# A convolution and an involution on one core: the pixel weights' layout, from [group, tap row] to [pair of groups, tap row, group of the pair]

## The chip, the cores and the metric

The kernel runs on one core of a Trainium2 chip. The metric is the device time of one execution in microseconds, the median of three runs. Names: PE is TensorE (PEld its weight load), DVE is VectorE, ACT is ScalarE, POOL is GpSimd, SP is the sync engine, which here only issues DMAs. SBUF is the on-chip memory of 128 partitions, PSUM the memory that matmuls write to, HBM (DRAM) the memory outside.

## The reference

The input `x` is [32, 256, 32, 32] in fp32: 32 images, 256 channels, 32 x 32 pixels. Two layers, each a group norm with 32 groups of 8 channels, an operator, and a residual:

```python
# layer 0: 3x3 convolution, 256 -> 256, on values rounded to fp16
x = x + _L0_conv_ref(_gn(x), L0_conv_weight, L0_conv_bias)
# layer 1: involution, K = 7, G = 16 groups of GC = 16 channels
y = relu(bn(einsum('oc,bchw->bohw', w1, xn)))            # 64 channels
w = einsum('oc,bchw->bohw', w2, y) + b2[None, :, None, None]
w = w.reshape(b, G, K * K, H, W)                          # 16 x 49 weights for each pixel
out = einsum('bgkhw,bgckhw->bgchw', w, patches)           # 7 x 7 patches, zero padded
x = x + out
```

In the involution each pixel has its own 49 weights for each of the 16 groups, and the 16 channels of a group share them.

## The kernel before

**Layer 0.** `front(b)` is a generator with the steps of one image: the group norm's sums (L219, ACT) and its small DVE operations (L227 to L235), the convolution as 18 fp16 matmuls for each half of the pixels and each half of the channels (L332), rounding to fp16 on DVE (L346), bias and residual (L348), the second group norm, the 64 channels `y` (L380, L387), and sixteen transposes of 128 x 128 (L395), copied into `pixels` by ACT (L399).

**The pixel weights.** `weights(b, r0)` makes the 7 x 7 x 16 weights of four image rows. With 32 columns of `y` as the stationary operand, a matmul (L410) gives the weights of 32 pixels: 16 groups for two tap columns `dj`, up to 224 numbers. Four of them, for different pairs of tap columns, fill 128 partitions. DVE then adds the bias `b2_sb` and writes the result from PSUM to the ring `w_sb` (L428); this is called the eviction here. The ring has one place for every output row, and in a place [group, tap row] with WIN = 10 tap rows, since an input row of a window of 4 rows can take part in 10 output rows. The place for a tap row depends on the row distance, so the eviction writes a diagonal: the offset `K1 - 1 - d0` and steps `[WB, rows], [WB - 1, d1 - d0], [WIN, G]`. The innermost step, over the groups, is WIN = 10 words. `ring_pieces` cuts an eviction where the ring wraps or the image ends, which gives the shapes of 224, 192, 128, 64 and 16 elements.

**The way through DRAM.** `scatter(b, k, part)` (L477, on SP) writes the ring's rows to `wd` in DRAM, 640 bytes for each pixel, row and tap column. In `wd` a pixel has WPIX = 7 * 160 + 4 words. `load_bands(b, k)` (L490) reads them back with partitions as input pixels: 16 DMAs for eight image rows, each of 16 rows of WPIX words; 14 are issued by POOL and two by SP. In the source, the row step `ROW - 1` shifts each row of pixels by one tap row, so that all pixels of a band line up. Three band buffers take turns.

**The sums.** `sums(b, m)` (L515) multiplies, for a window of 4 rows by 19 columns of pixels, `pixels` (stationary, 64 partitions x 32 channels, of which 16 are zero) with a slice of the band (moving), accumulating in `acc` in PSUM. For a group the moving operand is [19 pixels, up to 10 tap rows]; the 10 tap rows are adjacent words in SBUF and the pixels 160 words apart. Each fp32 matmul of the program runs as two MATMUL instructions, so a window takes 64. `add_windows` (L531, DVE) adds `acc` to `x`, and `store` (SP) writes the result.

**The order** is written out by hand: a loop over half-steps `n`, 16 for each image, in which sums, windows, weights (18 half-steps ahead), scatters, x loads and band loads (9 ahead) are placed by fixed distances. Each engine works its queue in that order.

Of the kernel before, what the change touches and what calls it, by code (L numbers as in the profile page):

```python
# [9 lines left out]
F32 = mybir.dt.float32  # L10
AF = mybir.ActivationFunctionType
ALU = mybir.AluOpType

P = 128
# [6 lines left out]
K1, PAD1 = 7, 3  # L21
TAPS = K1 * K1
CR = 64
G = 16
# [12 lines left out]
XR = 4  # L37
RG = 2
KP = P // RG
TR = RG * XR  # L40
SIDES = 2
JC = W // SIDES
K = H // TR
M = K * SIDES
WIN = XR + K1 - 1
WINC = JC + K1 - 1
WINI = JC + PAD1

WB = G * WIN
WPIX = K1 * WB + XR
SW = K1 * G
S = H + 2 * PAD1
T = 4
TW = P // T
PAIR = 3 * GC
PAIRS = G // 2
ROW = S * WPIX  # L60
WR = 4
NBAND = 3
SHARE = 8
NPIX = 6
RING = 24
# [6 lines left out]
def tile_quant_conv_then_involution(  # L72
# [16 lines left out]
    nc = tc.nc  # L89
    PSUM = bass.MemoryType.PSUM  # L90

    const = ctx.enter_context(tc.tile_pool(name="const", bufs=1))
# [45 lines left out]
        nc.gpsimd.memset(t, 0.0)  # L138

    y_sb = [const.tile([P, N // 2], F32, name=f"y_{i}") for i in range(2)]  # L140
    bands = [const.tile([P, SIDES, WINC * WB + XR], F32, name=f"band_{i}") for i in range(NBAND)]
    for t in bands[CH:]:
        nc.gpsimd.memset(t, 0.0)
    pixels = [const.tile([P, 2, PAIRS, PAIR], F32, name=f"pixels_{i}") for i in range(NPIX)]
# [1 line left out]
        nc.gpsimd.memset(t, 0.0)  # L146


    w_sb = const.tile([P, 2, RING, G, WIN], F32, name="w_sb")
    wd = dram.tile([H, S, WPIX], F32, name="wd")  # L150
    acc = [ps_acc.tile([P, RG, NT], F32, name=f"acc_{d}") for d in range(SIDES)]

# [6 lines left out]
    w2_sb = const.tile([P, K1, SW], F32, name="w2_sb")  # L159
    for i in range(2):  # L160
        nc.sync.dma_start(w2_sb[i * CR : (i + 1) * CR], w2)
    b2_sb = const.tile([P, 2, SW], F32, name="b2_sb")
    for dj in range(K1):
        t, e = divmod(dj, 2)
        nc.sync.dma_start(b2_sb[t * TW : (t + 1) * TW, e], b2[dj].partition_broadcast(TW))

    bias_sb = const.tile([P, CH], F32, name="bias_sb")
    nc.sync.dma_start(bias_sb, bias0.rearrange("(h p) -> p h", p=P))
# [15 lines left out]


    for col, cols, at, n in (
        (0, S, K1 * WB, XR),
        (PAD1, PAD1, 0, PAD1 * WB),
        (W, PAD1, (K1 - PAD1) * WB, PAD1 * WB),
    ):  # L190
        to = bass.AP(
            tensor=wd.tensor,
            offset=wd.offset + col * WPIX + at,
            ap=[[ROW, H], [WPIX, cols], [1, n]],
        )
        nc.sync.dma_start(to, bands[NBAND - 1][:H, 0, :n].unsqueeze(1).to_broadcast([H, cols, n]))
# [205 lines left out]
    def weights(b, r0):  # L402

        pws = [ps_w.tile([P, 2, 2, SW], F32, tag=f"pw{i}", name=f"pw{i}") for i in range(2)]
        for r in range(2):
            for t in range(T):
                for i in range(2):
                    half = slice(i * CR, (i + 1) * CR)
                    dj = slice(2 * t, min(2 * t + 2, K1))
                    nc.tensor.matmul(  # L410
                        pws[i][t * TW : (t + 1) * TW, r, : dj.stop - dj.start],
                        y_sb[b % 2][half, (r0 // 2 + r) * W : (r0 // 2 + r + 1) * W],
                        w2_sb[half, dj],
                        start=True,
                        stop=True,
                    )
        for i in range(2):
            for e in range(2):
                p = P if e == 0 else (K1 // 2) * TW
                for r, rows, d0, d1, at in ring_pieces(b, r0 + 2 * i):  # L420

                    to = w_sb[:p, e]
                    to = bass.AP(
                        tensor=to.tensor,
                        offset=to.offset + at * WB + K1 - 1 - d0,
                        ap=[to.ap[0], [WB, rows], [WB - 1, d1 - d0], [WIN, G]],
                    )
                    nc.vector.tensor_tensor(  # L428
                        to,
                        pws[i][:p, r : r + rows, e, d0 * G : d1 * G].rearrange("p r (d g) -> p r d g", g=G),  # L430
                        b2_sb[:p, e, d0 * G : d1 * G]
                        .unsqueeze(1)
                        .to_broadcast([p, rows, (d1 - d0) * G])
                        .rearrange("p r (d g) -> p r d g", g=G),
                        ALU.add,
                    )

    def ring_pieces(b, r0):

        def place(r, d):
            s = r0 + r + d - PAD1
            return (b * H + s) % RING if 0 <= s < H else None

        def together(d):
            return place(0, d) is not None and place(1, d) == place(0, d) + 1

        pieces = []
        for rows, ok in (  # L450
            ((0, 2), together),
            ((0, 1), lambda d: place(0, d) is not None and not together(d)),
            ((1, 1), lambda d: place(1, d) is not None and not together(d)),
        ):
            d = 0
            while d < K1:
                d0 = d
                while d < K1 and ok(d) and place(rows[0], d) == place(rows[0], d0) + d - d0:
                    d += 1
                if d > d0:  # L460
                    pieces.append((*rows, d0, d, place(rows[0], d0)))
                else:
                    d += 1
        return pieces

    def scatter(b, k, part):

        at = (b * H + k * TR) % RING
        for dj in range(part, K1, 2):
            t, e = divmod(dj, 2)  # L470
            to = bass.AP(
                tensor=wd.tensor,
                offset=wd.offset + k * TR * ROW + dj * WPIX + (K1 - 1 - dj) * WB,
                ap=[[WPIX, TW], [ROW, TR], [1, WB]],
            )
            rows = w_sb[t * TW : (t + 1) * TW, e, at : at + TR]
            nc.sync.dma_start(to, rows.rearrange("p s g r -> p s (g r)"))  # L477

    def load_bands(b, k):

        band = bands[(b * K + k) % NBAND]
        for i in range(JC):
            j = i // 2 + i % 2 * JC // 2
            src = bass.AP(
                tensor=wd.tensor,
                offset=wd.offset + k * TR * ROW + (j + PAD1) * WPIX,
                ap=[[ROW - 1, TR], [JC * WPIX, SIDES], [1, WPIX]],
            )
            queue = nc.sync if i % SHARE == SHARE - 1 else nc.gpsimd
            queue.dma_start(band[j::JC, :, j * WB : j * WB + WPIX], src)  # L490

    def windows(b, m):


        k, d = divmod(m, SIDES)
        for g in range(RG):
            top = k * TR + g * XR - PAD1
            at = acc[d][:, g, : CH * WINI * WIN].rearrange("p (h j r) -> p h j r", h=CH, r=WIN)
            yield g, at, top, max(top, 0), min(top + WIN, H)

    def sums(b, m):

        k, d = divmod(m, SIDES)
        j0 = 0 if d else PAD1
        band = bands[(b * K + k) % NBAND][:, d]
        px = pixels[(b * K + k) % NPIX][:, d]
        for h in range(CH):
            for v in range(2):
                for g, at, top, f, l in windows(b, m):
                    p = slice(g * KP, (g + 1) * KP)  # L510
                    of = band[p, g * XR + j0 * WB : g * XR + (j0 + WINI) * WB]
                    of = of.rearrange("p (j g r) -> p j g r", g=G, r=WIN)
                    for t in range(T):
                        a = h * T + t
                        nc.tensor.matmul(  # L515
                            at[t * TW : (t + 1) * TW, h, :, f - top : l - top],
                            px[p, a, v * GC : v * GC + TW],
                            of[:, :, 2 * a + v, f - top : l - top],
                            start=(h, v) == (0, 0),
                            stop=(h, v) == (CH - 1, 1),  # L520
                        )
# [20 lines left out]
    def due(n, lag):  # L542

        b, i = divmod(n - lag, per)
        return (b, i) if 0 <= b < B else (None, None)

    with tc.manual_schedule():
        fronts = {}
        for n in range(FRONT, B * per + 2):
            b, i = due(n, FRONT)  # L550
# [12 lines left out]
            b, i = due(n, 0)  # L563
            if b is not None and i % 2 == 0:
                sums(b, i // 2)
            b, i = due(n, 1)
# [6 lines left out]
            b, i = due(n, 2)  # L573
            if b is not None and i == 2 * (M - 1 - SIDES):
                store(b, 0)
            b, i = due(n, -LEAD)
            if b is not None and i % 2 == 0:
                weights(b, i // 2 * WR)

            for part in range(2):  # L580
                b, i = due(n, -LEAD + 1 + part)
                if b is not None and i % 2 == 0:
                    for k in range(K):
                        if i // 2 == min((k + 1) * TR // WR, H // WR - 1):
                            scatter(b, k, part)
            b, i = due(n, LOAD)
# [3 lines left out]
            b, i = due(n, 3 - 4 * NBAND)  # L590
            if b is not None and i % 4 == 0:
                load_bands(b, i // 4)
# [37 lines left out]
```

## Time and profile before

| | |
|---|---|
| median of three runs | 1392.44 us |
| lowest, highest | 1381.25, 1393.82 us |
| profiled execution, span from first to last instruction | 1387.9 us |
| busy in the span: PE, DVE, ACT, POOL | 1250.5, 934.7, 727.6, 1007.6 us |
| DMA, mean rate | 266 GB/s, 369 MB |
| evictions (L428): busy, count | 455.5 us, 1920 |
| sums (L515): busy, count | 411.6 us, 16,384 |

The profile is of one execution, whose own time is given only as its span. "Busy" counts time in which an engine had an instruction at work; instructions of one engine can overlap, so the mean duration of a group times its count can exceed its busy time. A group's row has, after the bar, busy time, mean duration in ns, and the idle time just before, with what ended it. A row of waits reads: engine, operation and line, what ended the wait, total us, times, longest us. "issue" is time in which the engine waited for nothing that the profile shows.

### The profile page before, as it was taken

What the parts mean: (1) busy time and instruction counts of PE and PEld (TensorE: products, weight loads), DVE (VectorE), ACT (ScalarE), POOL (GpSimd) and SP (SyncE); (2) the same over time, 40 slices, a digit from 0 to 9 for tenths busy, and PEclk for the clock granted to TensorE, in tenths of its full rate; (3) what the DMA queues carried; (4) which work ended last, traced back from release to release, by engine and by line L of the source; (5) the groups of instructions that cost most, each with busy time, mean ns of one, the idle gap of its engine ahead of it and who ended that gap; (6) DMA issues with size and microseconds to landing.
All of it is one profiled execution on the core that took longest, in us unless ns stands there. A gap on an engine that the chain in (4) does not pass through costs nothing.

```text
span 1387.9 us, 70012 instructions
## 1 busy us (share of the span) xinstructions
PE 1250.5 (90%) x29440; PEld 798.5 (58%) x29440; DVE 934.7 (67%) x3179; ACT 727.6 (52%) x1699; POOL 1007.6 (73%) x1818
## 2 busy tenths in 40 slices
PE   2899999899899999998899999899999999999665
PEld 1356555566565665655565666566566655666543
DVE  4467776677767776776576677667777776677652
ACT  4866555465645555655455555545565654653300
POOL 8057777777787777767777787776876777778785
PEclk9999999999999999999999999999999999999986
DMA  6079999999999998999999999999999999999995
GB/s 217 1 195 286 283 277 283 284 266 292 287 277 274 287 294 254 285 279 269 273 275 286 289 275 279 288 277 264 288 283 272 295 285 279 280 280 272 280 269 162
DMA packets 366232, 369.33 MB, mean 266 GB/s; under 512 B 78624, under 2 KB 308192, under 8 KB 365664
## 3 DMA queue, kind: packets, MB, share of 16 engines
q1 hardware_dynamic: 279904, 235.72, 57.5%
q0 software_dynamic: 86016, 129.14, 33.8%
q8 instruction: 234, 3.83, 1.2%
q14 instruction: 78, 0.64, 0.1%
HBM read 183.81 MB, written 180.74 MB: 263 GB/s over the span
## 4 chain that ended last, share of the span: by engine, by line
PE 55%; DMA 25%; DVE 5%; issue 5%; POOL 4%; SPq 3%; ACT 3%; POOLq 0%; DVEq 0%; ACTq 0%
PE pc L332 22%; PE acc L515 17%; DMA band<-wd 14%; PE pw L410 10%; DMA wd<-w_sb 8%; POOL band L490 4%; PE py L380 3%; DVE w_sb L428 3%; SPq L477 3%; PE pt L395 2%; DMA out<-x 1%; ACT junk L219 1%; DVE x L531 1%; DMA band<-in_w 1%; ACT xn L278 0%
## 5 line engine op out<-in xcount | busy, mean ns | idle before, releaser
L490 POOL DMA_DIRECT2D band<-wd x1792 | 978.0, 548 | 364.1 <-DMA band<-wd 225.3
L428 DVE TENSOR_TENSOR w_sb<-pw,b_sb 128x16 f32<-128x16 f32 (+9 forms) x1920 | 455.5, 349 | 359.2 <-PE pw L410 345.4
L332 PE MATMUL pc<-xq,wq 128*128 128x496 f16 (+3 forms) x2304 | 536.4, 379 | 32.5 <-ACT xq L278 28.0
L515 PE MATMUL acc<-band,pixels 64*32 64x190 f32 (+1 forms) x16384 | 411.6, 322 | 80.2 <-DMA band<-wd 44.6
L332 PEld LDWEIGHTS <-wq 128*128 128x128 f16 x2304 | 206.8, 98 | 328.2 <-issue 113.0
L515 PEld LDWEIGHTS acc<-band,pixels 64*32 64x32 f32 x16384 | 296.1, 108 | 165.1 <-issue 100.1
L410 PE MATMUL pw<-w_sb,y 64*32 64x224 f32 (+1 forms) x8192 | 291.2, 332 | 15.1 <-issue 13.9
L531 DVE TENSOR_TENSOR x<-acc,x 128x380 f32<-128x380 f32 (+1 forms) x512 | 261.7, 511 | 33.6 <-PE acc L515 24.6
L410 PEld LDWEIGHTS pw<-w_sb,y 64*32 64x32 f32 x8192 | 180.6, 106 | 45.7 <-issue 28.8
L399 ACT COPY pixels<-pt 128x512 f32<-128x512 f32 x128 | 73.6, 575 | 224.0 <-PE pt L395 224.0
L219 ACT ACTIVATE junk<-x 128x512 f16<-128x512 f32 (+1 forms) x192 | 146.5, 763 | 18.0 <-DVE x L348 9.6
L219 ACT ACTIVATE junk<-x,mean 128x1024 f16<-128x1024 f32 x128 | 147.1, 1149 | 4.3
L250 ACT ACTIVATE s<-back,eps 128x2 f32<-128x2 f32 x64 | 18.9, 296 | 207.3 <-DVE back L235 207.2
L346 DVE TENSOR_SCALAR q<-pc 128x512 f16<-128x512 f32 x128 | 87.2, 682 | 19.2 <-PE pc L332 19.0
L278 ACT ACTIVATE xn<-x,off,rstd 128x512 f32<-128x512 f32 x128 | 96.1, 800 | 0.0
L348 DVE SCALAR_TENSOR_TENSOR x<-q,bias_sb,x 128x512 f32<-128x512 f16 x128 | 92.0, 719 | 0.2
L395 PEld LDWEIGHTS pt<-ident,xn 128*128 128x128 f32 x512 | 63.9, 142 | 27.7 <-issue 3.3
L395 PE MATMUL pt<-ident,xn 128*128 128x128 f32 x512 | 78.0, 275 | 1.5 <-ACT pixels L399 1.5
L240 ACT ACTIVATE mean<-back 128x2 f32<-128x2 f32 x64 | 12.7, 198 | 120.6 <-DVE back L235 120.6
L278 ACT ACTIVATE xq<-x,off,rstd 128x1024 f16<-128x1024 f32 x64 | 75.5, 1226 | 0.0
L380 PEld LDWEIGHTS py<-xn,w_sb 128*64 128x64 f32 x2048 | 62.7, 138 | 16.7 <-issue 8.3
L380 PE MATMUL py<-xn,w_sb 128*64 128x64 f32 x2048 | 67.5, 224 | 2.8 <-ACT xn L278 1.8
(40 smaller groups left out, 374.5 us busy)
## 6 DMA issues: line engine op xcount, KB each, us to landing
wd<-w_sb SPq DMA_DIRECT2D x896, 160.0 KB
band<-wd POOLq DMA_DIRECT2D x1792, 70.2 KB, 4.9
x<-in_x SPq DMA_DIRECT2D x64, 512.0 KB
out<-x SPq DMA_DIRECT2D x64, 512.0 KB
band<-wd SPq DMA_DIRECT2D x256, 70.2 KB
band<-in_w SPq DMA_DIRECT2D x2, 1152.0 KB
w_sb<-in_w SPq DMA_DIRECT2D x2, 196.0 KB
wd<-band SPq DMA_DIRECT2D x2, 180.0 KB
```

What stands on the lines that cost most here:

```text
L219: nc.scalar.activation(junk[:, n0:n1], src[:, h, n0:n1], func, bias=bias, accum_out=self.sums[:, i : i + 1])
L278: nc.scalar.activation(dst, src, AF.Identity, bias=self.off[:, one], scale=self.rstd[:, one])
L332: nc.tensor.matmul(pc.rearrange("p (r c) -> p r c", c=W)[:, r0 - nt * RT : r1 - nt * RT, c0:c1], wq[:, kh, k, mh * P : (mh + 1) * P], xq[: ...
L346: nc.vector.tensor_scalar(q, pc, F16_MAX, -F16_MAX, ALU.min, ALU.max)
L348: nc.vector.scalar_tensor_tensor(xt[:, mh, cols], q, bias_sb[:, mh : mh + 1], xt[:, mh, cols], ALU.add, ALU.add)
L380: nc.tensor.matmul(py[i * CR : (i + 1) * CR, cols], w1_sb[:, kh, :], px[:, r : r + 2], start=kh == 0, stop=kh == CH - 1,)
L395: nc.tensor.transpose(pt[:, i, h * P : (h + 1) * P], xn[:, h, (m + i) * P : (m + i + 1) * P], ident)
L410: nc.tensor.matmul(pws[i][t * TW : (t + 1) * TW, r, : dj.stop - dj.start], y_sb[b % 2][half, (r0 // 2 + r) * W : (r0 // 2 + r + 1) * W], w ...
L428: nc.vector.tensor_tensor(to, pws[i][:p, r : r + rows, e, d0 * G : d1 * G].rearrange("p r (d g) -> p r d g", g=G), b2_sb[:p, e, d0 * G : d ...
L490: queue.dma_start(band[j::JC, :, j * WB : j * WB + WPIX], src)
L515: nc.tensor.matmul(at[t * TW : (t + 1) * TW, h, :, f - top : l - top], px[p, a, v * GC : v * GC + TW], of[:, :, 2 * a + v, f - top : l - top],
L531: nc.vector.tensor_tensor(x_at, of, x_at, ALU.add)
```

## The change

In `w_sb`, `wd` and the bands, the 160 numbers of a place are no longer [16 groups, 10 tap rows] but [8 pairs of groups, 10 tap rows, 2 groups of the pair]. So:

- The eviction's innermost step is two adjacent words; its loops are rows and pairs together, tap rows, and the two groups. For that, the matmul L410 writes its rows to other places in PSUM (row inside tap column), the host reorders the columns of `w2` and `b2` by pair, tap row, group, and the bias is held twice, once for each row, which takes 14 loads of `b2` where there were seven.
- One tap row is now two words, so the shift between rows in `load_bands` is `ROW - V` with V = 2, the band's second half of the partitions starts V * XR words in, and the padding grows from 4 to 8 words: a pixel has 1128 words in place of 1124.
- The sums read one group of a pair: the 10 tap rows are every second word.

```diff
+V = 2
+A = G // V
 WB = G * WIN
-WPIX = K1 * WB + XR
+PAD = V * (TR - XR)
+WPIX = K1 * WB + PAD
...
-    w_sb = const.tile([P, 2, RING, G, WIN], F32, name="w_sb")
+    w_sb = const.tile([P, 2, RING, A, WIN, V], F32, name="w_sb")
...
-    b2_sb = const.tile([P, 2, SW], F32, name="b2_sb")
+    b2_sb = const.tile([P, 2, 2, SW], F32, name="b2_sb")
     for dj in range(K1):
         t, e = divmod(dj, 2)
-        nc.sync.dma_start(b2_sb[t * TW : (t + 1) * TW, e], b2[dj].partition_broadcast(TW))
+        for r in range(2):
+            nc.sync.dma_start(b2_sb[t * TW : (t + 1) * TW, e, r], b2[dj].partition_broadcast(TW))
...
-                        pws[i][t * TW : (t + 1) * TW, r, : dj.stop - dj.start],
+                        pws[i][t * TW : (t + 1) * TW, : dj.stop - dj.start, r],
...
-                        ap=[to.ap[0], [WB, rows], [WB - 1, d1 - d0], [WIN, G]],
...
+                    evict(pws[i][:p, e, r : r + rows], e, r, rows, d0, d1, at)
+
+    def evict(of, e, r, rows, d0, d1, at):
+
+        p = of.shape[0]
+        to = w_sb[:p, e]
+        to = bass.AP(
+            tensor=to.tensor,
+            offset=to.offset + at * WB + V * (K1 - 1 - d0),
+            ap=[to.ap[0], [V * WIN, rows * A], [WB - V, d1 - d0], [1, V]],
+        )
+        of = of.rearrange("p r (a d v) -> p (r a) d v", a=A, v=V)
+        bias = b2_sb[:p, e, r : r + rows].rearrange("p r (a d v) -> p (r a) d v", a=A, v=V)
+        nc.vector.tensor_tensor(to, of[:, :, d0:d1], bias[:, :, d0:d1], ALU.add)
...
-                ap=[[ROW - 1, TR], [JC * WPIX, SIDES], [1, WPIX]],
+                ap=[[ROW - V, TR], [JC * WPIX, SIDES], [1, WPIX]],
...
-                    of = band[p, g * XR + j0 * WB : g * XR + (j0 + WINI) * WB]
-                    of = of.rearrange("p (j g r) -> p j g r", g=G, r=WIN)
+                    of = band[p, V * g * XR + j0 * WB : V * g * XR + (j0 + WINI) * WB]
+                    of = of.rearrange("p (j a r v) -> p j a r v", a=A, r=WIN, v=V)
...
-                            of[:, :, 2 * a + v, f - top : l - top],
+                            of[:, :, a, f - top : l - top, v],
```

More of the change, by code (lines that the diff above doesn't have):

```diff
@@ L140, in tile_quant_conv_then_involution @@
     y_sb = [const.tile([P, N // 2], F32, name=f"y_{i}") for i in range(2)]
-    bands = [const.tile([P, SIDES, WINC * WB + XR], F32, name=f"band_{i}") for i in range(NBAND)]
+    bands = [const.tile([P, SIDES, WINC * WB + PAD], F32, name=f"band_{i}") for i in range(NBAND)]
     for t in bands[CH:]:
@@ L186, in tile_quant_conv_then_involution @@
     for col, cols, at, n in (
-        (0, S, K1 * WB, XR),
+        (0, S, K1 * WB, PAD),
         (PAD1, PAD1, 0, PAD1 * WB),
@@ L420, in weights @@
                 for r, rows, d0, d1, at in ring_pieces(b, r0 + 2 * i):
[L422 to L425, printed above, removed]
-                        ap=[to.ap[0], [WB, rows], [WB - 1, d1 - d0], [WIN, G]],
[L427 to L436, printed above, removed]
+                    evict(pws[i][:p, e, r : r + rows], e, r, rows, d0, d1, at)
[10 more added lines that the diff above has]
+        nc.vector.tensor_tensor(to, of[:, :, d0:d1], bias[:, :, d0:d1], ALU.add)
     def ring_pieces(b, r0):
@@ L476, in scatter @@
             rows = w_sb[t * TW : (t + 1) * TW, e, at : at + TR]
-            nc.sync.dma_start(to, rows.rearrange("p s g r -> p s (g r)"))
+            nc.sync.dma_start(to, rows.rearrange("p s a r v -> p s (a r v)"))
     def load_bands(b, k):
@@ L603 @@
     v = {name: np.asarray(a) for name, a in inputs.items()}
-    w2 = v["L1_conv_w2"].reshape(G, K1, K1, CR).transpose(3, 2, 1, 0).reshape(CR, K1, K1 * G)
-    b2 = v["L1_conv_b2"].reshape(G, K1, K1).transpose(2, 1, 0).reshape(K1, K1 * G)
+    w2 = v["L1_conv_w2"].reshape(A, V, K1, K1, CR).transpose(4, 3, 0, 2, 1).reshape(CR, K1, K1 * G)
+    b2 = v["L1_conv_b2"].reshape(A, V, K1, K1).transpose(3, 0, 2, 1).reshape(K1, K1 * G)
     laid_out = {
```

## The prediction

> **What bounds the kernel now.** I read the page first: busy shares, the slices, the DMA queues.
>
> ```profile
> PE 1250.5 (90%) x29440; PEld 798.5 (58%) x29440; DVE 934.7 (67%) x3179; ACT 727.6 (52%) x1699; POOL 1007.6 (73%) x1818
> ...
> DMA  6079999999999998999999999999999999999995
> ...
> q1 hardware_dynamic: 279904, 235.72, 57.5%
> q0 software_dynamic: 86016, 129.14, 33.8%
> ```
>
> TensorE is at 90%, but from the fourth slice to the second last the DMA engines show a 9 too: the row of digits is as flat as PE's. So I asked for the busy time of the steady stretch alone.
>
> ```profile
> 220.00:1330.00 1110.00, 1036.08 (x25018) 667.47 (x25009) 774.75 (x2671) 593.24 (x1386) 834.91 (x1531) 0.99 0.97 280
> ```
>
> The columns are PE, PEld, DVE, ACT, POOL, clock, DMA share, GB/s. Two resources have nothing left: DMA (0.97) and PE, which idles 1110 - 1036.08 = 73.9 us, 6.7%. VectorE, whose work the change makes cheaper, idles 335 us. Who ends PE's idle time there, from the waits of the same stretch:
>
> ```profile
> PE acc L515 <- DMA band<-wd: 23.9, 17, 3.1
> ...
> PE acc L515 <- issue: 17.7, 20, 2.5
> PE pw L410 <- issue: 12.5, 19, 1.9
> ...
> PE acc L515 <- DMA wd<-w_sb: 6.4, 3, 3.9
> PE acc L515 <- DVE x L531: 4.9, 4, 2.2
> ...
> PE acc L515 <- DVE q L346: 1.5, 1, 1.5
> ...
> PE pw L410 <- DVE w_sb L428: 1.0, 3, 0.5
> ```
>
> Transfers end 30 us of it, unexplained "issue" another 30 us, VectorE only 4.9 + 1.5 + 1.0 = 7.4 us. The chain of waits agrees (DMA band 14%, wd 8%, POOL 4%, SP 3%, the eviction on VectorE 3%).
>
> [...] The rows by shape:
>
> ```profile
> L428 DVE TENSOR_TENSOR w_sb<-pw,b_sb 128x224 f32<-128x224 f32 x256 | 142.0, 555 | 166.0 <-PE pw L410 162.5 <-DMA wd<-w_sb 3.4
> ...
> L531 DVE TENSOR_TENSOR x<-acc,x 128x380 f32<-128x380 f32 x384 | 207.8, 541 | 26.1 <-PE acc L515 19.4
> ...
> L428 DVE TENSOR_TENSOR w_sb<-pw,b_sb 128x16 f32<-128x16 f32 x384 | 53.8, 176 | 0.0
> ...
> L531 DVE TENSOR_TENSOR x<-acc,x 128x266 f32<-128x266 f32 x128 | 53.9, 421 | 7.5 <-PE acc L515 5.2
> ```
>
> The eviction, whose output steps 40 bytes at every element, costs (555 - 176) / (224 - 16) = 1.82 ns an element; L531, also fp32 from PSUM with two sources, but written in runs of 19, (541 - 421) / (380 - 266) = 1.05 ns.
> [...] No matmul of the trace before reads fp32 with a step[...].
> [...] A pixel grows from 4496 to 4512 bytes, so every 640-byte scatter now starts on a multiple of 32, where half did not. The trace speaks against a price at the DMA engine: its packet records have 72% of the 640-byte packets at exactly 32 ns, more than the aligned half.
>
> **The change, part by part.**
> *Evictions (L428).* Still 1920, same pieces. Elements from the shapes: 512 x 224 + 256 x 192 + 256 x 128 + 128 x 64 + 768 x 16 = 217,088. At 1.05 instead of 1.82 ns they save 0.77 x 217,088 = 167 us of VectorE: L428 from 455.5 to about 288 us, a group of four from 1.75 to 1.06 us, the 224 shape from 555 to about 385 ns. Bounds: nothing (PSUM or bias reads hold it back) to 167; I take 167. On the path lies little of it: the 7.4 us for which PE waited for VectorE; of the scatter's own wait (6.4 us in three stalls, each behind an eviction, SP, a landing and a reload) some 2 us; one group at the start, 0.7 us. Sum at most 10 us. What covers the other 157 us is the full DMA: a scatter issued 0.7 us sooner joins a queue that is 97% busy. PE next waits for bands.
> *Sums (L515).* 16,384 matmuls, same counts, moving operand with a step of 8 bytes. One window's 64 matmuls hold PE for about 1.31 us (the timeline before a wait: sums begin at 760.32, L410's first at 761.63), 256 windows make 335 us. Bounds: nothing[...], to the trace's nearest row for a hop at each element, 1.82/1.05 = 1.74 times, +248 us; below nothing has no mechanism. I take nothing: each fp32 matmul streams slowly (190 elements in 332 ns, 1.7 ns each)[...].
> *Band loads (L490).* 2048 loads, 16 rows each, 16 bytes longer: 0.52 MB of 369 MB, 0.14%; if DMA is the bound all of it counts, 2 us. Same number of issues on POOL and SP. Alignment: nothing by the packet records; bounds -40 us (the 4496-byte packets average 242 ns against 174 for the commonest duration, and a third of that excess, 68 x 32,768 / 16 / 3 = 46 us of engine time, could go[...]) to +20 us (a pitch that meets worse in HBM).
> *Matmuls of L410* write the same 224 columns as two pieces of 112; nothing, by the equal counts.
> *Prologue.* Seven more bias loads on SP, ahead of bias_sb, w1, the bn vectors, the padding and the next x tiles. The seven there take 10.1 us, of which 6.8 wait for weights, so 3.3 us for seven more. x for image 1 is issued at 22.05 and read at 32.6, so the delay hides; if it didn't, 3 us. I take 0.5. No wait is added, so nothing queues behind one.
>
> *Sum* against the execution's span of 1387.9 us: -7.4 - 2 - 0.7 + 2 + 0.5 = -7.6, 1380 us. What lies around the span isn't shown; the median of the runs is 1392.4, 4.5 us above it, the fastest run 1381.3. On the median that is 1384.8. As the DMA may take part of it back (the same sum with only the start's gain gives +1.8, 1394), I say **1386**.
>
> **The rivals.**
> *B, the transfers get cheaper too.* [...] evictions that end sooner let SP issue more evenly. For it: DMA is the co-bound, and packets run far over their commonest duration. Against: the flat 32 ns. The -40 us bound, without the +2 us, makes A's 1384.8 about 1343; at half that size, 1363. I take 1355.
> *C, the strided operand slows the sums (the other side).* [...] PE has 73.9 us of idle in 1110, about 83 over the images. It decides from 83/335 = 25% slower sums on; at 40%, +134 - 83 + some 7 of stalls that remain makes 1450; at 74% about 1555. [...] Against: the slow fp32 stream[...].
> *D, the new pitch slows the band loads:* +20 us, 1412. Nothing in the profile speaks for it.
> *E, the evictions don't get faster:* 1394, inside A's range.
>
> **How the numbers follow.** A (hidden gain, with E): 0.42, range 1373 to 1400. B: 0.28, 1338 to 1378. C: 0.22, 1406 to 1560. D: 0.08. About 1% (1378.5 to 1406.4) is what a measurement of this kernel tells from no change, its three runs spreading over 0.9%. Faster by over 1%: nearly all of B, 0.26, and 0.07 of A, 0.33. Slower: C and most of D, 0.28. Same: 0.39. For the range I leave out C above 1450 (0.11) and B's lowest third (0.09): **1350 to 1450**.
>
> **What would show it.** Evictions: the 224 shape near 385 ns, L428 near 288 us. Sums: a window's stretch still 1.3 us, the 190 shape still 332 ns; C would show both longer and PE over 95% busy. DMA: share 0.97 unchanged and 640-byte packets still at 32 ns (A), a shorter mean of the long packets (B). The waits: PE on VectorE gone, PE on bands the same. I am wrong if the sums stretch, or if the transfers' mean duration moves.

## The result, and the profile after

The changed kernel takes 1383.28 us (median of 20 runs) where the kernel before, measured again beside it, takes 1393.88 us (20 runs): a ratio of 0.9931, 95% interval 0.9912 to 0.9949. That is 9.6 us less on 1393.88 by the ratio. The forecast was 1386. (Ratios, here and below, are of fast runs alone, those within 1.5% of the fastest of the same kernel, and differ by up to 0.2% from the quotient of the two medians.)

The profiled execution of the changed kernel took 1388.26 us with a span of 1386.5 us; 1.8 us lie around the span. It is one of the longer runs, so the two spans, 1387.9 and 1386.5, hardly differ: this pair of traces does not show the gain, only the repeated runs do. What the traces show is each part's own cost.

Busy shares, slices and queues of the changed kernel:

```profile
PE 1265.7 (91%) x29440; PEld 809.6 (58%) x29440; DVE 861.2 (62%) x3179; ACT 727.1 (52%) x1699; POOL 1010.0 (73%) x1818
...
DMA  6089999999999999999999999999999999999995
...
q1 hardware_dynamic: 280240, 235.90, 57.6%
q0 software_dynamic: 86016, 129.60, 33.8%
```

VectorE's busy time fell by 73 us, PE's rose by 15 us, the transfers look the same. In the steady stretch (us; busy of PE, PEld, DVE, ACT, POOL; clock, DMA share, GB/s) and in its waits:

```profile
220.00:1330.00 1110.00, 1050.05 (x24965) 677.59 (x24963) 716.36 (x2662) 592.38 (x1385) 831.61 (x1525) 0.99 0.97 280
```

```profile
PE acc L517 <- DMA band<-wd: 20.2, 13, 3.3
...
PE acc L517 <- issue: 11.5, 15, 3.0
PE acc L517 <- DMA wd<-w_sb: 5.5, 1, 5.5
...
PE acc L517 <- DVE x L533: 1.6, 3, 1.0
PE acc L517 <- DVE q L350: 1.6, 2, 0.9
...
PE pw L414 <- DVE w_sb L438: 1.0, 2, 0.6
```

DMA is at 0.97 and 280 GB/s as before. PE's waits for VectorE are 4.2 us in place of 7.4, in single traces (plain_sums below, with the same fast evictions, has 11.6, so that is no gain that can be counted on). PE idles 60 us in place of 73.9, but it got through no more matmuls in the same time (24,965 against 25,018): it idles less because its own work is longer. The groups by shape:

```profile
L517 PE MATMUL acc<-band,pixels 64*32 64x190 f32 x12288 | 424.4, 337 | 52.4 <-DMA band<-wd 32.1 <-issue 9.9 <-DMA wd<-w_sb 5.5
...
L438 DVE TENSOR_TENSOR w_sb<-pw,b_sb 128x224 f32<-128x224 f32 x256 | 98.1, 383 | 187.8 <-PE pw L414 184.7 <-DMA wd<-w_sb 3.0
...
L438 DVE TENSOR_TENSOR w_sb<-pw,b_sb 128x16 f32<-128x16 f32 x384 | 52.2, 164 | 0.0
```

The eviction's slope is now (383 - 164) / (224 - 16) = 1.05 ns an element, as forecast (383 against 385 ns). The sums' 190 shape went from 332 to 337 ns, and a window's stretch on PE from 1.31 to 1.39 us:

```profile
728.04 1.64 PE L517 MATMUL acc<-band,pixels 64*32 64x190 f32 x64 [1.39 <-DMA band<-wd]
729.43 0.98 PE L414 MATMUL pw<-w_sb,y 64*32 64x224 f32 x32
```

(728.04 to 729.43; the 1.39 in brackets is the idle time before.)

### The profile page after: what moved, and what is told of

Read it like the earlier page. It is cut to its first block, busy times and chain, and to the rows that moved or that the text cites. A ratio compares the mean times of both kernels' runs of the same rounds, so it can differ in the third digit from the quotient of the medians.

```text
span 1386.5 us, 70020 instructions
## 1 busy us (share of the span) xinstructions
PE 1265.7 (91%) x29440; PEld 809.6 (58%) x29440; DVE 861.2 (62%) x3179; ACT 727.1 (52%) x1699; POOL 1010.0 (73%) x1818
## 4 chain that ended last, share of the span: by engine, by line
PE 58%; DMA 24%; POOL 5%; issue 4%; DVE 3%; ACT 3%; SPq 2%; POOLq 0%; DVEq 0%; ACTq 0%
PE pc L336 22%; PE acc L517 19%; DMA band<-wd 13%; PE pw L414 11%; DMA wd<-w_sb 9%; POOL band L492 5%; PE py L384 3%; PE pt L399 3%; DVE w_sb L438 2%; ACT junk L223 1%; SPq L479 1%; DMA w_sb<-in_w 1%; DVE x L533 0%; ACT xn L282 0%; DMA x<-in_x 0%
## 5 line engine op out<-in xcount | busy, mean ns | idle before, releaser
L438 DVE TENSOR_TENSOR w_sb<-pw,b_sb 128x16 f32<-128x16 f32 (+9 forms) x1920 | 373.7, 265 | 423.9 <-PE pw L414 403.5
L517 PE MATMUL acc<-band,pixels 64*32 64x190 f32 (+1 forms) x16384 | 427.1, 330 | 68.5 <-DMA band<-wd 45.8
L517 PEld LDWEIGHTS acc<-band,pixels 64*32 64x32 f32 x16384 | 301.7, 106 | 157.9 <-issue 86.1
L414 PEld LDWEIGHTS pw<-w_sb,y 64*32 64x32 f32 x8192 | 187.7, 106 | 48.3 <-issue 31.1
```

Source lines behind the costliest of these rows:

```text
L414: nc.tensor.matmul(pws[i][t * TW : (t + 1) * TW, : dj.stop - dj.start, r], y_sb[b % 2][half, (r0 // 2 + r) * W : (r0 // 2 + r + 1) * W], w ...
L438: nc.vector.tensor_tensor(to, of[:, :, d0:d1], bias[:, :, d0:d1], ALU.add)
L517: nc.tensor.matmul(at[t * TW : (t + 1) * TW, h, :, f - top : l - top], px[p, a, v * GC : v * GC + TW], of[:, :, a, f - top : l - top, v], ...
```

## The experiments

My theory, A: the gain comes from VectorE, and the full DMA hides most of it. The rival, B: it comes from the starts of the scatters, which the eight words of padding put on multiples of 32 bytes. Each kernel was timed beside the kernel before on the same chip, with 6 to 22 runs of its own.

| kernel | median us | before beside it | ratio | 95% interval |
|---|---|---|---|---|
| before_again | 1394.49 | 1395.11 | 0.9997 | 0.9969 to 1.0026 |
| pad_only | 1382.13 | 1395.11 | 0.9907 | 0.9872 to 0.9943 |
| slow_evict | 1390.26 | 1395.11 | 0.9967 | 0.9946 to 0.9988 |
| plain_sums | 1386.50 | 1395.11 | 0.9931 | 0.9909 to 0.9953 |
| pitch1128 | 1381.29 | 1391.00 | 0.9932 | 0.9910 to 0.9953 |
| pitch1132 | 1394.65 | 1391.00 | 1.0015 | 0.9992 to 1.0039 |
| pitch1152 | 1368.67 | 1391.00 | 0.9857 | 0.9816 to 0.9898 |
| late_bias | 1381.67 | 1391.00 | 0.9944 | 0.9925 to 0.9964 |
| shift16 | 1481.43 | 1393.73 | 1.0631 | 1.0584 to 1.0678 |
| pairs1132 | 1392.07 | 1393.73 | 0.9989 | 0.9960 to 1.0019 |
| pairs1152 | 1369.51 | 1393.73 | 0.9837 | 0.9800 to 0.9875 |
| group4 | 1622.93 | 1393.73 | 1.1662 | 1.1620 to 1.1705 |

### The kernel before again

> The kernel before, unchanged, for the spread of a pair that should be equal and for a second trace of its start. Every theory: ratio 1.000, within 0.003. The start differs in the two traces that we have: the two quantising operations of VectorE took 5.4 us each before and 1.9 us each after, and the first convolution began at 24.8 and 19.7 us. If that comes from the layout, this run shows 5.4 us again and the first convolution near 25 us; if it is chance (whichever of VectorE and POOL's memset comes first), it may show 1.9 us and about 20 us in the same kernel.

The ratio is 1.000, and the start is chance. The quantising operations of VectorE in the first trace of this kernel, and in this one:

```profile
9.27 10.97 DVE L201 TENSOR_SCALAR wq<-band 128x2304 f16<-128x2304 f32 x2 [1.66 <-DMA band<-in_w]
```

```profile
8.43 1.84 DVE L201 TENSOR_SCALAR wq<-band 128x2304 f16<-128x2304 f32 x1 [0.79 <-DMA band<-in_w]
11.49 1.36 DVE L201 TENSOR_SCALAR wq<-band 128x2304 f16<-128x2304 f32 x1 [1.22 <-DMA band<-in_w]
```

They took 1.84 and 1.36 us here; the 10.97 us of the first trace are 3.73 and 7.11 us. The steady stretch has 276 GB/s in this trace and 280 in the first, which is how far two traces of one kernel can lie apart. The first sums start at 89.8 us here, at 97.4 in the first trace, at 93.9 in the changed kernel. So the start says nothing about the change.

### The padding alone

```diff
-WPIX = K1 * WB + XR
+PAD = 2 * XR
+WPIX = K1 * WB + PAD
...
-    bands = [const.tile([P, SIDES, WINC * WB + XR], F32, name=f"band_{i}") for i in range(NBAND)]
+    bands = [const.tile([P, SIDES, WINC * WB + PAD], F32, name=f"band_{i}") for i in range(NBAND)]
...
-        (0, S, K1 * WB, XR),
+        (0, S, K1 * WB, PAD),
```

> The kernel before with pixels of 1128 words in place of 1124, nothing else. Theory A (the gain comes from VectorE): 1.000 to 1.002, as only 0.14% more bytes move. Theory B[...]: 0.993, the whole gain, with a shorter mean of the long packets.

0.9907: four words of padding, with the old order of the weights, the old evictions and the old sums, give as much as the whole change. Theory A falls as the account of the gain. The sign that B gave, a shorter mean of the long packets, did not show: the long packets average 243 ns in this trace, 242 and 247 in the two of the kernel before.

### The pairs with slow evictions

```diff
-            ap=[to.ap[0], [V * WIN, rows * A], [WB - V, d1 - d0], [1, V]],
+            ap=[to.ap[0], [V * WIN, rows * A], [1, V], [WB - V, d1 - d0]],
...
-        nc.vector.tensor_tensor(to, of[:, :, d0:d1], bias[:, :, d0:d1], ALU.add)
+        swap = "p r d v -> p r v d"
+        nc.vector.tensor_tensor(to, of[:, :, d0:d1].rearrange(swap), bias[:, :, d0:d1].rearrange(swap), ALU.add)
```

> The changed kernel with the eviction's loops swapped, so that its innermost step is 158 words again; same layout, sums, transfers and result. Theory A: the 224 shape goes back to 555 ns or more and the gain goes with it, and as the sums stay strided the time ends at 1.000 to 1.012 of the kernel before. Theory B, or a gain of the start: stays at 0.993 to 0.996.

The 224 shape takes 582 ns (555 before the change, 383 after), and half of the gain goes: 0.9967 against 0.9931. The two intervals just meet, so an eviction of 383 ns in place of 582 gives 0.36%, 5 us, with an uncertainty of about the same size. As 582 ns is also slower than the kernel before was, not all of this is a gain on that kernel. Neither theory's forecast fits alone.

### The pairs with contiguous sums

```diff
-                    of = of.rearrange("p (j a r v) -> p j a r v", a=A, r=WIN, v=V)
+                    of = of.rearrange("p (j g r) -> p j g r", g=G, r=WIN)
...
-                            of[:, :, a, f - top : l - top, v],
+                            of[:, :, 2 * a + v, f - top : l - top],
```

> The changed kernel with the sums reading ten adjacent words, as before, out of the new layout; the tap rows and groups that they then take are not the right ones, so this part of the computation differs. It prices the 8-byte step. The traces put it at 1.39 us for a window against 1.31, 0.08 x 256 = 20 us of PE. If PE is as much the bound as DMA, the time falls by up to 20 us more, to 0.980 to 0.985; if DMA is the bound, little, 0.990 to 0.993. A window should take 1.31 us again.

The price on PE is as put down: a window takes 1.31 us again (727.24 to 728.55), and the shape is back at 329 ns:

```profile
L517 PE MATMUL acc<-band,pixels 64*32 64x190 f32 x12288 | 409.1, 329 | 49.1 <-DMA band<-wd 24.8 <-issue 10.4 <-DVE q L350 6.7
```

The time does not move: 0.9931, the same as with strided sums. In the steady stretch PE is busy 13 us less and idles 13 us more than in the changed kernel (73.2 and 60.0 us). The extra idle time is spread over transfers, VectorE and "issue"; the waits for bands alone went down, from 20.2 to 9.3 us. So PE's own work is not what sets the time here.

### Is it the start of the writes, the length of the reads, or the pitch?

Three kernels with the old weights' order that differ only in the distance of two pixels in DRAM; the loads keep 1124 words, the bands their places.

```diff
-WPIX = K1 * WB + XR
+READ = K1 * WB + XR
+WPIX = 1128
...
-        (0, S, K1 * WB, XR),
+        (0, S, K1 * WB, WPIX - K1 * WB),
...
-                ap=[[ROW - 1, TR], [JC * WPIX, SIDES], [1, WPIX]],
+                ap=[[ROW - 1, TR], [JC * WPIX, SIDES], [1, READ]],
...
-            queue.dma_start(band[j::JC, :, j * WB : j * WB + WPIX], src)
+            queue.dma_start(band[j::JC, :, j * WB : j * WB + READ], src)
```

> The kernel before with pixels 1128 words apart in DRAM (every scatter starts on a multiple of 32 bytes), but loads of 1124 words into the old bands. B1, the 32-byte starts of the writes bring the gain: 0.990 to 0.993, as with the padded pixel. B2, the loads' length of 4512 bytes and their aligned places in SBUF bring it: 1.000.

> The same with 1132 words (4528 bytes): half of the scatters start 16 bytes off a multiple of 32 again, as before, but the pitch is another one. B1: 1.000. B3, the old pitch was a bad one for HBM whatever the alignment: 0.990 to 0.993 here too.

> The same with 1152 words (4608 bytes, 18 x 256): every scatter starts on a multiple of 128 bytes. B1: 0.990 to 0.993, and lower, 0.980 to 0.988[...]. B2: 1.000. B3: no forecast, between 0.985 and 1.01.

1128 words: 0.9932, the whole gain without a longer load or another place in the bands, so B2 falls. 1132 words, half of the starts off again: 1.0015, so it is not that any other pitch would do (B3). 1152 words, starts on multiples of 128 bytes: 0.9857, twice the gain. For the gain from 1124 to 1128 words the reads can't be what is aligned: in the old order their rows are shifted by 4 bytes each, so one row start in eight lies on 32 bytes with either pitch. Counted over all row starts of an image, from the start of `wd`, their spread over the 4-byte places within 32, 64, 128, 256 and 512 bytes is the same with 1124, 1128 and 1132 words. With 1152 words it is the same only within 32 bytes, so for the second half of the gain the reads, or this pitch itself, are not ruled out. The steady stretch with 1152 words:

```profile
220.00:1330.00 1110.00, 1044.99 (x25440) 673.28 (x25438) 786.19 (x2715) 593.13 (x1384) 849.88 (x1558) 0.99 0.96 284
```

284 GB/s and 25,440 matmuls in the time in which the two traces of the kernel before did 280 and 276, 25,018 and 24,818.

### All starts off, not half

```diff
+SHIFT = 4
...
-    wd = dram.tile([H, S, WPIX], F32, name="wd")
+    wd = dram.tile([H + 1, S, WPIX], F32, name="wd")
...
-                offset=wd.offset + k * TR * ROW + dj * WPIX + (K1 - 1 - dj) * WB,
+                offset=wd.offset + SHIFT + k * TR * ROW + dj * WPIX + (K1 - 1 - dj) * WB,
```

(Of the kernel with 1128 words; the loads and the padding move along.)

> The kernel with pixels 1128 words apart, all of wd moved on by 16 bytes, so that every scatter, not half of them, starts 16 bytes off a multiple of 32. B1, the starts of the writes: as far above the kernel before as all-aligned was below it, 1.004 to 1.010. Were it the pitch of 4512 bytes, 0.993 as without the shift.

1.0631: the sign is as B1 has it, the size nine times what I put down. Same instructions, same bytes, same pitch as the kernel at 0.9932; only the 16 bytes differ, and the one more row that `wd` needs for them. The rate shows it, first with 1128 words, then shifted:

```profile
220.00:1330.00 1110.00, 1043.63 (x25285) 671.43 (x25274) 782.00 (x2700) 596.48 (x1389) 840.51 (x1542) 0.99 0.98 281
```

```profile
220.00:1330.00 1110.00, 1000.67 (x23476) 634.51 (x23460) 731.68 (x2537) 574.85 (x1347) 776.90 (x1425) 0.99 0.97 263
```

The chain that ended last turns from PE to DMA: first the kernel before (its second trace has PE 44%, DMA 33%), then the shifted one.

```profile
PE 55%; DMA 25%; DVE 5%; issue 5%; POOL 4%; SPq 3%; ACT 3%; POOLq 0%; DVEq 0%; ACTq 0%
```

```profile
DMA 45%; PE 31%; POOL 8%; issue 7%; DVE 5%; ACT 3%; SPq 1%; POOLq 0%; DVEq 0%; ACTq 0%
```

The loads move by the same 16 bytes, and no run here moved writes and reads apart. But the spread of their row starts, counted as above, is the same with the shift as without it, so it is the writes whose alignment changed. Why the second half of the starts costs so much more than the first is open, and so is whether the longer `wd` lies elsewhere in DRAM, as no trace shows its address.

The packet records of the traces (no view of the page prints them) show where the time went: mean durations, and their sum over 16 engines.

| kernel | 640-byte writes, ns | share at just 32 ns | band rows, ns | both, us per engine |
|---|---|---|---|---|
| before / before_again | 36.1 / 36.0 | 72.5% / 72.4% | 241.9 / 247.5 | 1012 / 1024 |
| pitch1128 | 35.9 | 75.5% | 241.0 | 1008 |
| pitch1152 | 35.2 | 83.1% | 231.2 | 979 |
| shift16 | 38.3 | 75.1% | 256.3 | 1074 |

Between the best and the worst starts the reads beside the writes change (231 to 256 ns) as well as the writes (35.2 to 38.3 ns). The commonest duration of a write is 32 ns in all five traces. The gain of 0.7% does not stand out in these sums: 1008 us with 1128 words, where the two equal kernels have 1012 and 1024. Nor do longer packets alone show a bad start: the last kernel below, with all starts on multiples of 64 bytes and a less busy DMA, has 37.5 and 252.6 ns.

### The pairs without and with the alignment

The edit in both is that of the 1128-word kernel, made in the changed kernel, with `READ = K1 * WB + PAD` and 1132 or 1152 words.

> The changed kernel, pairs of groups and all, with pixels 1132 words apart in DRAM, so that half of the scatters start off the 32 bytes as before: the pair layout without the alignment. If the alignment is all of the gain: 1.000 (0.998 to 1.003). If the faster eviction gave part of it: 0.995 to 0.998. If the strided sums and the bias loads cost more than the eviction gives: above 1.003.

> The changed kernel with pixels 1152 words apart, scatters on multiples of 128 bytes. With the transfers relieved, PE is nearer to being the bound, so the slower sums (20 us of PE) may show: 0.985 if the pairs are neutral as in the kernel with the 32-byte starts, 0.990 if the sums are now on the path, 0.980 if the earlier evictions now count.

0.9989 (0.9960 to 1.0019) without the alignment: the pairs alone are worth nothing that can be measured. Theory A's 7.6 us would have been 0.9945, outside this interval. With 1152 words 0.9837, against 0.9857 with the old order: the intervals overlap almost wholly. Both are faster than the changed kernel (0.9931), and the old order with 1152 words needs only the four edits above.

### The bias loads

```diff
+    def load_b2():
+        for dj in range(K1):
...
             if n == FRONT + CH:
                 quantize_weights()
+            if n == 1 - LEAD - TW // 2:
+                load_b2()
```

> The changed kernel with its 14 bias loads issued behind the x loads of image 1. In the traces the first sums come at 105 us with 14 loads ahead and at 101 us with seven (counting as the packet records do). If the seven more loads cost that at the start, 3.5 us fall away: 0.990 to 0.991 of the kernel before against 0.993, and the first sums come at 101 us or before. If that is chance: 0.993.

0.9944, no gain: the first sums start at 96.1 us. With a start that moves by 7.6 us in the same kernel, the price of the loads isn't shown either way.

### Groups of four: a step of 16 bytes

```diff
-V = 2
+V = 4
...
-                            of[:, :, a, f - top : l - top, v],
+                            of[:, :, (2 * a + v) // V, f - top : l - top, (2 * a + v) % V],
```

> The changed kernel with groups of four in place of pairs, so that the sums' moving operand steps 16 bytes[...]; a pixel has 1136 words, so scatters start on multiples of 64 bytes. The eviction writes runs of four: the 224 shape near 380 ns. [...] the sums stretch far: a window from 1.39 to 2 us or more, 256 x 0.6 = 150 us less PE's idle time of 60 us, 1.05 or above. If the 8-byte step's 6% was already the price of every step, a window of 1.4 to 1.5 us and 0.985 to 0.995.

1.1662. The groups by shape and the steady stretch:

```profile
L517 PE MATMUL acc<-band,pixels 64*32 64x190 f32 x12288 | 749.4, 514 | 11.2 <-DMA band<-wd 7.4 <-DMA wd<-w_sb 2.4 <-DVE w_sb L438 1.4
...
L438 DVE TENSOR_TENSOR w_sb<-pw,b_sb 128x224 f32<-128x224 f32 x256 | 98.3, 384 | 320.6 <-PE pw L414 320.6
```

```profile
220.00:1330.00 1110.00, 1109.84 (x20950) 636.01 (x20942) 605.50 (x2277) 518.36 (x1208) 695.01 (x1275) 1.00 0.84 236
```

The eviction stays at 384 ns, but the sums' shape goes from 337 to 514 ns, and a window to about 2.3 us (60 of its 64 matmuls alone take from 720.41 to 722.59). PE is busy without a gap (1109.84 of 1110 us) and DMA falls to 0.84. Runs of two are enough for the eviction (383 ns, against 384 with runs of four). The sums bear a step of 8 bytes (337 ns, against 332 before the change) and not one of 16 (514 ns); the reason is not shown.

## Why the prediction was right, and where it was not

The time and the sign are right; the account of the gain is not, and that the number came out is in the main luck. The sum had -10.1 us from VectorE, +2.5 from band length and prologue, and nothing from alignment: -7.6. The runs have -9 to -13 us from the padding or the pitch with nothing else changed, and between -5.6 and +2.6 us from the pairs without it.

**Bound and cover: right, the cover in part argued.** The evictions' busy time on VectorE fell by 82 us, and little of it reached the time. Evictions that are a third shorter give 5 us with the alignment (0.9967 to 0.9931, barely beyond noise), and the pairs without it nothing clear (0.9989). The forecast's "at most 10 us" was the ceiling, not the size. That PE is not the cover is shown by the contiguous sums, which took 20 us from PE and nothing from the time; that the transfers set it is shown by the pitch, which changed them alone. No run made the transfers much lighter to see the evictions' saving appear: with 1152 words the DMA share is still 0.96.

**Evictions: instruction right, sum wrong.** 383 ns against 385, summed durations from 670 to 508 us, 162 against 167. That runs of two words would cost the 1.05 ns an element of L531's runs of 19 was my estimate, which none of the prediction's rows shows. But the group's busy time fell only from 455.5 to 373.7 us, not to 288, and a group of four from 1.75 us to between 1.28 and 1.38, not to 1.06. The step that failed is the subtraction of durations from busy time: instructions overlap, and before the change they overlapped more. In a group of four the spacing was (1.75 - 0.555) / 3 = 0.40 us, so 0.16 us of each lay under the next; after, with 1.28 us, it is 0.30 and 0.08. What counts is the spacing of the starts. The trace records give, for evictions that follow each other without a gap, a median of 401 ns at 224 elements and 70 ns at 16 before, 298 and 81 ns after: slopes of 1.59 and 1.04 ns an element, 0.55 apart and not 0.77, and a constant that rose by some 20 ns. An estimate from these is 217,088 x 0.00055 - 1920 x 0.020 = 81 us, and 82 were measured.

**Alignment of the band loads and scatters: the step that failed.** "Alignment: nothing by the packet records" should have read -13 to -9 us: padding alone gives 0.9907, the pitch alone 0.9932, and theory A's 7.4 us of waits are not needed for the result. The mistake was to read the price in the commonest duration of a packet, which is 32 ns with all starts off 32 bytes and with all on 128. Why the starts cost what they do was not shown. Rival B named the place, the transfers; its 20 to 40 us were two to four times too much.

**Sums: small price, hidden.** I took nothing, an estimate from the 332 ns for 190 elements; it is 0.08 us a window, 20 us of PE, 6%, and contiguous sums give none of it back (0.9931 in both). Rival C is real, one step further: with 16 bytes the busy time of the sums grows by 76% (427.1 to 751.1 us, from the changed kernel), and the time is 229 us above the kernel before; C's estimate for 74% was 1555 where the runs gave 1623.

**Prologue and band length: not settled.** 0.5 us and 2 us lie under a start that moves by 7.6 us and intervals of some 3 us.

## What to carry to other kernels

Where the transfers are the bound, look at the byte addresses at which small writes start in DRAM before you look at any engine: here a pitch alone gave 0.7% or 1.4% less time, and a shift of 16 bytes made it 6.3% more than before. A change of layout brings its padding along; price and test the padding alone. Don't take a packet's commonest duration as proof that its alignment is free: change the alignment alone and time it, as neither that duration nor the means of one trace showed the 0.7%. And where instructions overlap, work out a saving from the spacing of their starts, not from their durations: here the spacing gave 81 us and the durations 167, where 82 were measured.

## What the runs showed of the hardware that I had not expected

- Moving all of one DRAM buffer by 16 bytes, so that every 640-byte write starts 16 bytes off a multiple of 32, took the rate from 281 to 263 GB/s and the time from 0.9932 to 1.0631 of the kernel before; with half of the writes off it was 1.000.
- An fp32 matmul on 64 rows and 32 columns (64 of them in 1.31 us) slows from 332 to 337 ns with a moving operand of 8-byte steps, and to 514 ns with 16-byte steps.
- In two traces of one kernel the first sums come 7.6 us apart. The same two quantising operations of VectorE took 3.73 and 7.11 us in one, each ending 1.2 us after a memset of POOL had ended, and 1.84 and 1.36 us in the other, where two of POOL's memsets of `pixels` took 1.9 us in place of 0.73.
